# A window-attention and FFT-filter block on one core: attention weights divided ahead of the transpose, heads laid out by GpSimd's transfers

## The chip, the cores and the metric

The kernel runs on one core of a Trainium2 chip. The metric is the device time of one execution in microseconds (us); of several executions the median is given. A core has five engines that work side by side: TensorE (PE, matrix multiplications; PEld is its load of the stationary operand), VectorE (DVE), ScalarE (ACT), GpSimd (POOL) and SyncE (SP, which here only issues transfers). Everything is float32.

## What is computed

The input x has 8 images of 384 channels and 64x64 pixels. Two blocks follow each other, each added to its input:

```python
# block 1: windowed attention
xt = layernorm(groupnorm(x) as tokens of 384 channels) * norm_g + norm_b
qkv = xt @ qkv_w + qkv_b                       # q, k, v of 384 channels each
# channels 0..191: branch 0; channels 192..383: branch 1, the image rolled by (-4, -4)
# each branch: 8x8 windows of 64 tokens, 4 heads of 48 channels
attn = q @ k.T * 48**-0.5 + bias[head]         # branch 1: and a mask
out_b = softmax(attn) @ v                      # branch 1 is rolled back
x = x + concat(out_0, out_1) @ proj_w + proj_b
# block 2: filter
t = w_in @ groupnorm(x)                        # per pixel, 384 to 384
t = irfft2(rfft2(8x8 patches of t) * fft_filter)
t = depthwise_conv3x3(t, w_dw)
x = x + w_out @ (gelu(t[:192]) * t[192:])
```

The group norms need statistics over a whole image (32 groups of 12 channels).

## The kernel before

**Strips and units.** An image is cut into 8 strips of 8 rows, 512 tokens. A strip has two units, one for each branch (`br`), so an image has 16 units. The attention strip `s` of image `b` starts at unit u = 16b + 2s, its branch `br` at w = u + br. Block 2 of image b ("conv stage") runs beside the attention of image b+1: its strip s starts at u = 16(b+1) + 2 + 2s. For the last image nothing is left beside it, and this is the tail of the program.

**The plan.** A list of pieces is written by `at(place, piece, ...)` (L832 and after for attention), sorted by place, and run in that order. TensorE executes its instructions just as written (`keep_in_program_order` in the helpers `matmul`, L62, and `transpose`, L72). The instructions of the other engines are ordered by a scheduler when the program is built, within dependencies and the pins that the program sets (`behind`, `keep_in_program_order`). Empty instructions on TensorE (`nop`, counted in `FETCHES`, `WAITS` and `RUN_AT`) align the places at which instructions are fetched.

**PSUM.** Two pools: "gemm", four buffers of 128x512, and "att", two buffers of 128x2x512 (`psum2`). "att" is taken in turn by the scores pS, the transposed weights pT, the weighted values pA, the turned output po, and by pw2, the third output of `finish`. The matrix multiplication that first writes a buffer waits until the readers of its previous holder are done.

**One unit of attention, with the lines.**

- `group_normal` (L338, DVE) writes y; `ln_square` (L347) squares it on ACT into sq, and POOL adds the three parts of sq (L350); `ln_sums` sums over channels on PE, ACT and DVE turn the sums into factors (L362 to L367, among them ACT's Sqrt), these go through a line in DRAM and come back spread over all partitions as rs (L374, L376, SP's queue); `ln_scale` (L389, DVE) multiplies. POOL makes the half-shifted copy of y for branch 1 (L402 to L404).
- `qk_tile`: products pq, moved by ACT to qab, kab, qcd, kcd (L420). Heads lie at 64 rows each.
- `v_tile`: pvv, copied by ACT to v (L454). v has 49 columns per head, the last is set to one by POOL (L445).
- `scores`: pS, 32 products of 64x64. `weights` (DVE): bias added (L482), maximum (L486), subtraction (L489). `exponent` (ACT, L495). `turn`: eight transposes into pT, one ACT copy eT (L505).
- `apply`: eT stationary (64x64), v moving (49 columns): pA has tokens on its partitions, and the 49th column of each head is the sum of the weights. `normalise` (DVE): reciprocal of the sums (L529) and product o (L530).
- `put`: eight transposes of o into po (with the identity or one that swaps halves), and copies by ACT and DVE into oT, which has channels on partitions (L553, L554, L561 to L563; branch 1, the shifted one, goes in two halves to two strips).
- `project`: pr from oT and proj_w, added by DVE to x_add (L572). `keep` takes statistics (L247), `store` writes the result of block 1 to DRAM (SP).

**One strip of the conv stage.** `normal_x1` (ACT, L600), `mix` (pt, copied by ACT at L610), `transform` (pf, multiplied by the filter on DVE, L627), `back` (pz, 96 products). Then `border` once for each of three channel tiles: ACT copies pz into z, which has a border of one pixel (L655), and the border rows between neighbouring strips (L658 reads pz, L659 reads z). `conv`: nine taps; the first by ACT (L695), eight by DVE (L701, with zz as the running sum). `gate`: Gelu on ACT and products on DVE (L714 to L718). `finish`: products pw into two "gemm" buffers and pw2, in this order on PE, sixteen of 64 rows and then four of 128; DVE adds them to x_finish (L740 to L742), SP stores.

**The order around a finish.** On PE a strip's `back` (unit u + 1.99), the `apply` of branch 1 (w + 1.00), the next `scores` (w + 0.05) and a `finish` of an earlier conv strip (u + 6.10) follow each other: pz, pA, pS, pw. Of the "att" buffers, pS takes the one that pT held, pw2 the one that pA held.

Of the kernel before, what the change touches and what calls it, by code (L numbers as in the profile page):

```python
# [7 lines left out]
F32 = mybir.dt.float32  # L8
AF = mybir.ActivationFunctionType
ALU = mybir.AluOpType  # L10
# [17 lines left out]
C_SWAP = C_PICK + 2  # L28
N_CONST = C_SWAP + 128
WAITS = 5.325, -22  # L30
FETCHES = {"qk_tile": 12, "v_tile": 24, "project": 12, "scores": 128, "apply": 128, "turn": 16, "put": 16,
# [7 lines left out]
def block_kernel(ctx: ExitStack, tc: tile.TileContext, out, x, consts, fsel, wqk, wv, bqk, bv,  # L39
# [52 lines left out]
    swap = cst[:, C_SWAP:C_SWAP + P]  # L92
# [6 lines left out]
    nc.vector.memset(eps_t, LN_EPS)  # L99
    std_t = cp.tile([P, 1], F32, name="std_t")  # L100
# [193 lines left out]
    for z in z_bufs:  # L294
        nc.gpsimd.memset(z[:, :, 0:1], 0.0)
        nc.gpsimd.memset(z[:, :, SW + 1:SW + 2], 0.0)
    gs0, gs1, st0s, st1s, x1d = ({} for _ in range(5))

    def behind(i, other, kind, reason):
        tc.add_manual_dep(i.ins, other.ins.name, mybir.DependencyInfo(kind, mybir.DependencyReason.DATA),  # L300
                          reason=reason)

# [49 lines left out]
    def ln_sums(b, s):  # L352
# [10 lines left out]
        rc = sb.tile([P, P], F32, tag="lr", bufs=2, name=f"lr_{b}_{s}")  # L363
        nc.vector.tensor_tensor(rc, m[:, 0:P], m[:, 0:P], ALU.mult)  # L364
        nc.vector.tensor_tensor(rc, m[:, P:2 * P], rc, ALU.subtract)
        nc.scalar.activation(rc, rc, AF.Sqrt, bias=eps_t)
# [19 lines left out]
    def ln_scale(b, s):  # L386

        y, rs = ys[b, s], ys.pop((b, s, "rs"))
        nc.vector.tensor_tensor(y, y, rs.unsqueeze(1).to_broadcast([P, KC, ST]), ALU.mult)  # L389
# [50 lines left out]
    def v_tile(b, s, br, g):  # L440

        y = y2s[b, s] if br else ys[b, s]
        if g == 0:
            v = sb.tile([P, 4, 4, HD + 1], F32, tag="v", bufs=2, name=f"v_{b}_{s}_{br}")
            nc.gpsimd.memset(v[:, :, :, HD:HD + 1], 1.0)  # L445
            vs[b, s, br] = v
        v = vs[b, s, br]
        pvv = psum(f"pvv_{b}_{s}_{br}_{g}")
        for i in range(2):
            pair = 2 * g + i  # L450
            for k in range(KC):
                matmul(pvv[:, i * 192:(i + 1) * 192], y[:, k, pair * P:(pair + 1) * P],
                                 wv_sb[:, k, br * 192:(br + 1) * 192], start=(k == 0), stop=(k == KC - 1))
        nc.scalar.copy(v[:, 2 * g:2 * g + 2, :, 0:HD],  # L454
                       pvv[:, 0:384].rearrange("p (g h d) -> p g h d", g=2, h=4))
# [17 lines left out]
    def weights(b, s, br):  # L473
# [13 lines left out]
        if br == 0 and "added" in zs:  # L487
            behind(i, zs.pop("added"), mybir.DependencyClass.NoSync, "residual first")
        zs["soft"] = nc.vector.tensor_tensor(e, e, mx.unsqueeze(2).to_broadcast([P, 2 * NS, 64]),  # L489
                                             ALU.subtract)  # L490
        qks[b, s, br, "e"] = e

    def exponent(b, s, br):
        e = qks[b, s, br, "e"]
        nc.scalar.activation(e, e, AF.Exp)  # L495

# [11 lines left out]
    def apply(b, s, br):  # L508

        eT, v = qks.pop((b, s, br, "eT")), vs.pop((b, s, br))  # L510
        pA = psum2(f"pA_{b}_{s}_{br}")
        for i in range(2):
            for h in range(4):
                to = (i * 4 + h) * (HD + 1)
                for odd in range(2):
                    pair = 2 * i + odd
                    for q in range(2):
                        rows, half = slice(q * 64, (q + 1) * 64), (q + odd) % 2
                        col = pair * P + (h + q) % 2 * 64
                        matmul(pA[half * 64:(half + 1) * 64, odd, to:to + HD + 1],  # L520
                               eT[rows, h // 2, col:col + 64], v[rows, pair, h, :], start=True, stop=True)
        qks[b, s, br, "A"] = pA

    def normalise(b, s, br):
        nm = f"{b}_{s}_{br}"
        o = os_[b, s, br] = sb.tile([P, 2, 2, 192], F32, tag="o", bufs=1, name=f"o_{nm}")
        pA = qks.pop((b, s, br, "A"))[:, :, 0:8 * (HD + 1)].rearrange("p g (h d) -> p g h d", h=8)
        rc = small.tile([P, 2, 8], F32, tag="rc", bufs=2, name=f"rc_{nm}")
        nc.vector.reciprocal(rc.unsqueeze(3), pA[:, :, :, HD:HD + 1])  # L529
        nc.vector.tensor_tensor(  # L530
            o.rearrange("p g i (h d) -> p g (i h) d", d=HD),
            pA[:, :, :, 0:HD], rc.unsqueeze(3).to_broadcast([P, 2, 8, HD]), ALU.mult)
# [6 lines left out]

    def put(b, s, br):  # L540


        o = os_.pop((b, s, br))
        p = psum2(f"po_{b}_{s}_{br}")
        po = []
        for a in range(2):
            for pair in range(4):
                transpose(p[:, a, pair * P:(pair + 1) * P], o[:, pair % 2, pair // 2, a * 64:a * 64 + P],
                          swap if pair % 2 else ident)
            po.append(p[:, a].rearrange("p (w r c) -> p r w c", w=NS, r=WS))  # L550
        if br == 0:
            oT = out_tile(b, s)
            nc.scalar.copy(oT[:, 0].rearrange("p r (w c) -> p r w c", c=WS), po[0])  # L553
            nc.vector.tensor_copy(oT[64:P, 1].rearrange("p r (w c) -> p r w c", c=WS), po[1][64:P])  # L554
            return
        for half, oT in ((0, out_tile(b, s)), (1, out_tile(b, (s + 1) % NS))):
            to, of = slice(4 - 4 * half, 8 - 4 * half), slice(4 * half, 4 * half + 4)
            for rows, kt, src, copy in ((slice(0, 64), 1, po[0], nc.vector.tensor_copy),
                                        (slice(0, P), 2, po[1], nc.scalar.copy)):
                d = oT[rows, kt, to]  # L560
                copy(d[:, :, 4:60].rearrange("p r (w c) -> p r w c", c=WS), src[rows, of, 0:7])  # L561
                copy(d[:, :, 60:64], src[rows, of, 7, 0:4])
# [408 lines left out]
```

## Time and profile before

The time before is 3689.26 us, the median of 3 runs (3688.66 to 3691.13). The profiled execution took 3687.27 us; its span, from the first to the last instruction in the trace, is 3685.3 us, and TensorE's granted clock was 0.996 of full speed. The figures below are of this one execution.

| from the views of the profile | value |
| --- | --- |
| profiled execution, span | 3687.27 us, 3685.3 us |
| window 1500 to 2000 us: PE busy | 496.86 us |
| the same: DVE, ACT, POOL busy | 399.99, 336.88, 59.62 us |
| DVE zz L701 | 1483 instructions, 1076.1 us, mean 751 ns |
| DVE x_add L572 | 192, 143.4 us, mean 747 ns |
| ACT oT L553, 128x512 | 64, 37.5 us, mean 585 ns |
| ACT z L655 | 192, 125.9 us, mean 672 ns |
| ACT loads of a function table | 72 counted at L495, 92.4 us, mean 1283 ns |
| POOL DMA issue L175, 2 KB | 64, 35.8 us, mean 582 ns; 5.5 us from issue to landing |

How to read the lines of the profile: a group has the source line, the engine, the operation, what it writes and from what, partitions x elements and type, and the number of records (a float32 product that isn't a transpose leaves two on PE); after the bar the busy time in us and the mean of one in ns; after the second bar the engine's idle time just before the group and what ended most of it. In the timeline the columns are the start in us, the length in us, the group and, in brackets, the idle time before it and what ended it. Matrix products are pipelined, so their lengths overlap: what a group costs is read from its start to the start of the next. In the view of waits a line has engine, operand and line of the waiting instruction, what it waited for, and the sum, the number and the longest of the waits.

### The profile page before, as it was taken

What the parts mean: (1) busy time and instruction counts of PE and PEld (TensorE: products, weight loads), DVE (VectorE), ACT (ScalarE), POOL (GpSimd) and SP (SyncE); (2) the same over time, 40 slices, a digit from 0 to 9 for tenths busy, and PEclk for the clock granted to TensorE, in tenths of its full rate; (3) what the DMA queues carried; (4) which work ended last, traced back from release to release, by engine and by line L of the source; (5) the groups of instructions that cost most, each with busy time, mean ns of one, the idle gap of its engine ahead of it and who ended that gap; (6) DMA issues with size and microseconds to landing.
All of it is one profiled execution on the core that took longest, in us unless ns stands there. A gap on an engine that the chain in (4) does not pass through costs nothing.

```text
span 3685.3 us, 92936 instructions
## 1 busy us (share of the span) xinstructions
PE 3610.8 (98%) x38598; PEld 2340.3 (64%) x38598; DVE 2836.7 (77%) x4601; ACT 2382.5 (65%) x3947; POOL 426.1 (12%) x764
## 2 busy tenths in 40 slices
PE   6999999999999999999999999999999999999998
PEld 4666666666666666666666666666666666666554
DVE  5655578778878788877888778878788777777898
ACT  3776576667666576666766766666676666676442
POOL 4111011101111011111111111111011111100000
PEclk8999999999999999999999999999999999999999
DMA  4232223223323133323332322323232322221432
GB/s 121 87 101 81 76 96 126 85 90 121 124 90 106 70 133 123 105 81 118 118 107 93 112 97 104 133 81 110 87 130 102 109 90 85 100 82 69 159 112 78
DMA packets 144355, 377.07 MB, mean 102 GB/s; under 512 B 12288, under 2 KB 12876, under 8 KB 143948
## 3 DMA queue, kind: packets, MB, share of 16 engines
q1 hardware_dynamic: 139952, 370.60, 28.5%
q8 instruction: 319, 5.23, 0.6%
q0 software_dynamic: 2048, 0.15, 0.1%
q10 hardware_dynamic: 1948, 0.37, 0.1%
q14 instruction: 88, 0.72, 0.1%
HBM read 270.28 MB, written 100.79 MB: 101 GB/s over the span
## 4 chain that ended last, share of the span: by engine, by line
PE 86%; DVE 6%; DMA 3%; ACT 2%; issue 1%; ACTq 0%; SPq 0%; DVEq 0%
PE pq L62 25%; PE pr L62 13%; PE pvv L62 12%; PE pt L62 12%; PE pw L62 6%; DVE zz L701 3%; PE pS L62 3%; PE pA L62 3%; PE po L72 3%; PE pT L72 3%; PE pz L62 3%; PE pf L62 2%; PE ln L62 2%; DMA x_norm<-in_x_dram 1%; DMA rs<-line 1%
## 5 line engine op out<-in xcount | busy, mean ns | idle before, releaser
L701 DVE SCALAR_TENSOR_TENSOR zz<-z,dw_sb,zz 128x512 f32<-128x512 f32 x1483 | 1076.1, 751 | 23.1 <-ACT z L658 11.0
L62 PE MATMUL pq<-y,wqk_sb 128*128 128x512 f32 x2160 | 990.1, 596 | 0.0
L62 PEld LDWEIGHTS pq<-y,wqk_sb 128*128 128x128 f32 x2160 | 402.3, 190 | 436.6 <-issue 403.4
L62 PE MATMUL pt<-wi_sb,xn 128*128 128x384 f32 x1536 | 535.0, 486 | 1.0 <-ACT xn L600 1.0
L62 PE MATMUL pr<-oT,wp_sb 128*128 128x512 f32 x1152 | 523.1, 592 | 0.9 <-DVE oT L563 0.9
L62 PE MATMUL pvv<-wv_sb,y 128*128 128x192 f32 x2880 | 495.8, 326 | 0.0
L62 PEld LDWEIGHTS pvv<-wv_sb,y 128*128 128x128 f32 x2880 | 471.7, 190 | 36.2 <-issue 22.2
L420 ACT ACTIVATE qab<-pq,bq_sb,cst 96x512 f32<-96x512 f32 (+1 forms) x256 | 197.8, 773 | 383.0 <-PE pq L62 381.1
L62 PEld LDWEIGHTS pt<-wi_sb,xn 128*128 128x128 f32 x1536 | 285.9, 190 | 202.7 <-issue 43.3
L420 ACT ACTIVATE kcd<-pq,vec 32x512 f32<-32x512 f32 x512 | 348.4, 680 | 9.0
L62 PEld LDWEIGHTS pr<-oT,wp_sb 128*128 128x128 f32 x1152 | 211.1, 190 | 224.3 <-issue 213.5
L402 POOL COPY y<-y 128x384 f32<-128x384 f32 x112 | 100.0, 893 | 1525.0 <-PE pvv L62 1020.5
L610 ACT COPY t<-pt 128x384 f32<-128x384 f32 x256 | 124.2, 485 | 186.0 <-PE pt L62 182.8
L364 DVE TENSOR_TENSOR lr<-m 128x128 f32<-128x128 f32 x64 | 18.9, 295 | 281.6 <-ACT m L362 281.6
L695 ACT ACTIVATE zz<-z,dw_sb 128x512 f32<-128x512 f32 x182 | 133.1, 733 | 151.0 <-PE pw L62 139.2
L350 POOL TENSOR_TENSOR sq<-sq 128x512 f32<-128x512 f32 x122 | 156.4, 1282 | 627.4 <-ACT sq L347 622.6
L420 ACT ACTIVATE qcd<-pq,bq_sb,cst 96x512 f32<-96x512 f32 (+1 forms) x256 | 197.1, 770 | 45.6 <-PE pq L62 42.1
L454 ACT COPY v<-pvv 128x384 f32<-128x384 f32 x256 | 120.8, 477 | 157.6 <-PE pvv L62 156.9
L572 DVE SCALAR_TENSOR_TENSOR x_add<-pr,vec,x_add 128x512 f32<-128x512 f32 x192 | 143.4, 747 | 93.3 <-PE pr L62 91.5
L62 PE MATMUL pw<-zz,wo_sb 128*128 128x512 f32 (+1 forms) x512 | 182.2, 499 | 0.0
L420 ACT ACTIVATE kab<-pq,vec 96x512 f32<-96x512 f32 (+1 forms) x256 | 174.1, 680 | 8.5 <-PE pq L62 6.8
L72 PEld LDWEIGHTS pT<-cst,e 128*128 128x128 f32 x1024 | 119.1, 141 | 67.8 <-issue 39.3
(142 smaller groups left out, 5292.4 us busy)
## 6 DMA issues: line engine op xcount, KB each, us to landing
x_add<-in_x_dram SPq DMA_DIRECT2D x64, 768.0 KB, 9.7
x1d<-x_add SPq DMA_DIRECT2D x64, 768.0 KB, 3.7
x_mix<-x1d SPq DMA_DIRECT2D x64, 768.0 KB, 4.6
x_finish<-x1d SPq DMA_DIRECT2D x64, 768.0 KB, 5.8
out_dram<-x_finish SPq DMA_DIRECT2D x64, 768.0 KB, 3.8
x_norm<-in_x_dram SPq DMA_DIRECT2D x61, 768.0 KB, 7.6
x_stats<-in_x_dram SPq DMA_DIRECT2D x56, 768.0 KB, 7.8
rs<-line SPq DMA_DIRECT2D x62, 256.0 KB, 3.0
```

The source lines that it names most:

```text
L62: tc.keep_in_program_order(nc.tensor.matmul(*args, **kw))
L72: tc.keep_in_program_order(nc.tensor.transpose(*args, **kw))
L350: nc.gpsimd.tensor_tensor(sq[:, 0, :], sq[:, 0, :], sq[:, k, :], ALU.add)
L364: nc.vector.tensor_tensor(rc, m[:, 0:P], m[:, 0:P], ALU.mult)
L402: nc.gpsimd.tensor_copy(dst[:, :, :, :, 0:4], src[:, :, :, :, 4:8])
L420: return nc.scalar.activation(dst[to:to + n], pq[of:of + n], AF.Identity, bias=bias[of:of + n], scale=scale)
L454: nc.scalar.copy(v[:, 2 * g:2 * g + 2, :, 0:HD], pvv[:, 0:384].rearrange("p (g h d) -> p g h d", g=2, h=4))
L572: nc.vector.scalar_tensor_tensor(t[:, m, :], pr, bp_sb[:, m:m + 1], t[:, m, :], ALU.add, ALU.add)
L610: nc.scalar.copy(t1, pt[:, 0:C])
L695: nc.scalar.activation(zz.rearrange("p (r c) -> p r c", c=SW), z[:, 1:9, 1:SW + 1], AF.Copy, scale=dw_sb[:, m, 4:5])
L701: i = nc.vector.scalar_tensor_tensor(acc.rearrange("p (r c) -> p r c", c=SW), z[:, dy:dy + 8, dx:dx + SW], dw_sb[:, m, TAPS[tap]:TAPS[tap] ...
```

## The change

- `divide` is new, on DVE after `exponent`: the sum over each row of e, its reciprocal, and the product. `normalise` is gone, and with it v's column of ones: v is contiguous, 768 columns and 16 of padding, in one fixed buffer per branch.
- `apply` makes v stationary (64 columns: the 48 of a head and 16 of what comes after it) and eT moving (64 columns). pA then has channels on its partitions, two heads per tile at rows 0 and 64. The 16 columns over give rows that nobody reads.
- `put` has no transposes. ACT copies pA into o (branch 0: two copies of 512 columns; branch 1: 512, 384, 64 and 64), and GpSimd issues transfers that move each head's 48 rows from o to their place in oT: five for branch 0, ten for branch 1, where a head may be cut at the edge of a tile.
- `border` is split: `inner` copies pz into z, for tiles 0 and 2 in `back`, for tile 1 in `borders` at u + 2.08, where all border rows are copied too, now both from z.
- Orders are fixed. `after_softmax` puts `ln_scale`, the sums of `project` and all taps of `conv` (except for the last image) behind the newest softmax on DVE; `after_out` puts the border copies and the first tap on ACT behind the last o copy of a branch 1. A one-column Exp right after the Sqrt of `ln_sums` brings the table of Exp early.
- Places in the plan: exponent from 0.30 to 0.13, divide at 0.23 or 0.26, turn from 0.64 to 0.80, put from 1.23 to 1.07. The buffer lr is single. The swapping matrix is gone; `WAITS` has new numbers.

```diff
@@ -28,4 +28,3 @@
-C_SWAP = C_PICK + 2
-N_CONST = C_SWAP + 128
-WAITS = 5.325, -22
-FETCHES = {"qk_tile": 12, "v_tile": 24, "project": 12, "scores": 128, "apply": 128, "turn": 16, "put": 16,
+N_CONST = C_PICK + 2
+WAITS = 5.97, -31
+FETCHES = {"qk_tile": 12, "v_tile": 24, "project": 12, "scores": 128, "apply": 128, "turn": 16,
@@ -99,0 +98 @@
+    exp_t = cp.tile([P, 1], F32, name="exp_t")
@@ -296,0 +296,4 @@
+    v_bufs = [cp.tile([P, 16 * HD + 16], F32, name=f"v{i}") for i in range(2)]
+    for v in v_bufs:
+        nc.gpsimd.memset(v[:, 16 * HD:], 0.0)
@@ -302,0 +306,4 @@
+    def after_softmax(i):
+        if "soft" in zs:
+            behind(i, zs["soft"], mybir.DependencyClass.NoSync, "softmax first")
@@ -363 +370 @@
-        rc = sb.tile([P, P], F32, tag="lr", bufs=2, name=f"lr_{b}_{s}")
+        rc = sb.tile([P, P], F32, tag="lr", bufs=1, name=f"lr_{b}_{s}")
@@ -366 +373,3 @@
-        nc.scalar.activation(rc, rc, AF.Sqrt, bias=eps_t)
+        i = nc.scalar.activation(rc, rc, AF.Sqrt, bias=eps_t)
+        behind(nc.scalar.activation(exp_t, eps_t, AF.Exp), i, mybir.DependencyClass.NoSync, "table in time")
@@ -389 +398 @@
-        nc.vector.tensor_tensor(y, y, rs.unsqueeze(1).to_broadcast([P, KC, ST]), ALU.mult)
+        after_softmax(nc.vector.tensor_tensor(y, y, rs.unsqueeze(1).to_broadcast([P, KC, ST]), ALU.mult))
@@ -444,3 +454 @@
-            v = sb.tile([P, 4, 4, HD + 1], F32, tag="v", bufs=2, name=f"v_{b}_{s}_{br}")
-            nc.gpsimd.memset(v[:, :, :, HD:HD + 1], 1.0)
-            vs[b, s, br] = v
+            vs[b, s, br] = v_bufs[br]
@@ -454,2 +462 @@
-        nc.scalar.copy(v[:, 2 * g:2 * g + 2, :, 0:HD],
-                       pvv[:, 0:384].rearrange("p (g h d) -> p g h d", g=2, h=4))
+        nc.scalar.copy(v[:, 384 * g:384 * (g + 1)], pvv[:, 0:384])
@@ -489,2 +496,2 @@
-        zs["soft"] = nc.vector.tensor_tensor(e, e, mx.unsqueeze(2).to_broadcast([P, 2 * NS, 64]),
-                                             ALU.subtract)
+        zs.pop("soft", None)
+        nc.vector.tensor_tensor(e, e, mx.unsqueeze(2).to_broadcast([P, 2 * NS, 64]), ALU.subtract)
@@ -496,0 +504,7 @@
+    def divide(b, s, br):
+        e = qks[b, s, br, "e"]
+        rc = small.tile([P, 2 * NS], F32, tag="rc", bufs=2, name=f"rc_{b}_{s}_{br}")
+        nc.vector.tensor_reduce(rc, e, AX.X, ALU.add)
+        nc.vector.reciprocal(rc, rc)
+        zs["soft"] = nc.vector.tensor_tensor(e, e, rc.unsqueeze(2).to_broadcast([P, 2 * NS, 64]), ALU.mult)
@@ -512,10 +527,8 @@
-        for i in range(2):
-            for h in range(4):
-                to = (i * 4 + h) * (HD + 1)
-                for odd in range(2):
...
+        for hp in range(2):
+            for pair in range(4):
+                to = (hp * 4 + pair) * 64
+                for par, q in ((0, 0), (1, 1), (0, 1), (1, 0)):
+                    rows, of = slice(q * 64, (q + 1) * 64), (pair * 4 + hp * 2 + par) * HD
+                    col = pair * P + (par + q) % 2 * 64
+                    matmul(pA[par * 64:(par + 1) * 64, q, to:to + 64], v[rows, of:of + 64],
+                           eT[rows, hp, col:col + 64], start=True, stop=True)
@@ -524,10 +536,0 @@
-    def normalise(b, s, br):
-        nm = f"{b}_{s}_{br}"
-        o = os_[b, s, br] = sb.tile([P, 2, 2, 192], F32, tag="o", bufs=1, name=f"o_{nm}")
-        pA = qks.pop((b, s, br, "A"))[:, :, 0:8 * (HD + 1)].rearrange("p g (h d) -> p g h d", h=8)
...
@@ -539,0 +543,4 @@
+    def after_out(i):
+        if "out" in zs:
+            behind(i, zs["out"], mybir.DependencyClass.NoSync, "weighted values first")
@@ -543,8 +550,7 @@
-        o = os_.pop((b, s, br))
-        p = psum2(f"po_{b}_{s}_{br}")
-        po = []
-        for a in range(2):
...
+        pA = qks.pop((b, s, br, "A")).rearrange("p o (h w r c) -> p o h w r c", h=2, w=4, r=WS)
+        o = sb.tile([P, 2, ST], F32, tag="o", bufs=1, name=f"o_{b}_{s}_{br}")
+        def columns(first, n, step=16, c=WS):
+            return bass.AP(o.tensor, o.offset + first, [list(o.ap[0]), [ST, 2], [step, n], [SW, WS], [1, c]])
@@ -552,12 +558,19 @@
-            oT = out_tile(b, s)
-            nc.scalar.copy(oT[:, 0].rearrange("p r (w c) -> p r w c", c=WS), po[0])
-            nc.vector.tensor_copy(oT[64:P, 1].rearrange("p r (w c) -> p r w c", c=WS), po[1][64:P])
-            return
...
+            for q in range(2):
+                nc.scalar.copy(columns(q * WS, 4), pA[:, q])
+            parts = ((slice(0, WS), 0, out_tile(b, s)),)
+        else:
+            nc.scalar.copy(columns(4, 4), pA[:, 0])
+            nc.scalar.copy(columns(12, 3), pA[:, 1, :, 0:3])
+            nc.scalar.copy(columns(60, 1, c=4), pA[:, 1, :, 3:4, :, 0:4])
+            zs["out"] = nc.scalar.copy(columns(0, 1, c=4), pA[:, 1, :, 3:4, :, 4:8])
+            parts = ((slice(4, 8), 0, out_tile(b, s)), (slice(0, 4), 256, out_tile(b, (s + 1) % NS)))
+        edge = (P, 64)[br]
+        for rows, of, oT in parts:
+            n = (rows.stop - rows.start) * SW
+            for h in range(4):
+                row = h % 2 * 64 - h * HD
+                for a, z in ((h * HD, min((h + 1) * HD, edge)), (max(h * HD, edge), (h + 1) * HD)):
+                    if a < z:
+                        to = a + br * P + (64 if a >= edge else 0)
+                        nc.gpsimd.dma_start(out=oT[to % P:to % P + z - a, to // P, rows],
+                                            in_=o[row + a:row + z, h // 2, of:of + n])
@@ -572 +585,2 @@
-        nc.vector.scalar_tensor_tensor(t[:, m, :], pr, bp_sb[:, m:m + 1], t[:, m, :], ALU.add, ALU.add)
+        after_softmax(nc.vector.scalar_tensor_tensor(t[:, m, :], pr, bp_sb[:, m:m + 1], t[:, m, :],
+                                                     ALU.add, ALU.add))
@@ -644,2 +658,3 @@
-        for m in (0, 2, 1):
-            border(b, s, m, pz[m])
+        zs[b, s, "pz"] = pz
+        for m in (0, 2):
+            inner(b, s, m)
@@ -647 +662 @@
-    def border(b, s, m, pz):
+    def inner(b, s, m):
@@ -654,6 +669,2 @@
-        rows = by_window(pz)
-        nc.scalar.activation(z[:, 1:9, 1:SW + 1].rearrange("p r (w c) -> p w r c", c=WS), rows, AF.Copy)
-        if s:
-            above = zs[b, s - 1, m]
...
+        nc.scalar.activation(z[:, 1:9, 1:SW + 1].rearrange("p r (w c) -> p w r c", c=WS),
+                             by_window(zs[b, s, "pz"][m]), AF.Copy)
@@ -661,0 +673,8 @@
+    def borders(b, s):
+        inner(b, s, 1)
+        for m in (0, 2, 1) if s else ():
+            above, z = zs[b, s - 1, m], zs[b, s, m]
+            after_out(nc.scalar.copy(above[:, WS + 1, 1:SW + 1], z[:, 1, 1:SW + 1]))
+            after_out(nc.scalar.copy(z[:, 0, 1:SW + 1], above[:, WS, 1:SW + 1]))
@@ -695,2 +714,2 @@
-                nc.scalar.activation(zz.rearrange("p (r c) -> p r c", c=SW), z[:, 1:9, 1:SW + 1], AF.Copy,
-                                     scale=dw_sb[:, m, 4:5])
+                after_out(nc.scalar.activation(zz.rearrange("p (r c) -> p r c", c=SW), z[:, 1:9, 1:SW + 1],
+                                               AF.Copy, scale=dw_sb[:, m, 4:5]))
@@ -707,2 +726,2 @@
-        if b < B - 1 and (tap == 6 or m == 0 and tap == 1):
-            behind(i, zs["soft"], mybir.DependencyClass.NoSync, "softmax first")
+        if b < B - 1:
+            after_softmax(i)
@@ -797,2 +816,4 @@
-                at(w + 0.30, exponent, b, s, br)
-                at(w + 0.64, turn, b, s, br)
+                at(w + 0.13, exponent, b, s, br)
+                at(w + (0.23, 0.26)[br], divide, b, s, br)
+                at(w + 0.80, turn, b, s, br)
@@ -800,2 +821 @@
-                at(w + 1.07, normalise, b, s, br)
-                at(w + 1.23, put, b, s, br)
+                at(w + 1.07, put, b, s, br)
@@ -827,0 +848 @@
+            at(u + 2.08 if b < B - 1 or s < NS - 1 else u + 1.991, borders, b, s)
@@ -831 +852 @@
-                    at(u + (2.62, 3.15, 3.5)[n] + 0.06 * tap, conv, b, s, m, tap)
+                    at(u + (2.62, 3.10, 3.5)[n] + 0.05 * tap + (0.4 if n == 2 and tap > 3 else 0), conv, b, s, m, tap)
```

## The prediction, made before the changed kernel was run

> **What bounds the kernel now.** I read the page's busy line and chain first, then the lines by shape (who does the removed and added work), then the waits between 500 and 3430 us (the repeating part), last the timeline at one finish.
>
> ```profile
> PE 3610.8 (98%) x38598; PEld 2340.3 (64%) x38598; DVE 2836.7 (77%) x4601; ACT 2382.5 (65%) x3947; POOL 426.1 (12%) x764
> PE 86%; DVE 6%; DMA 3%; ACT 2%; issue 1%; ACTq 0%; SPq 0%; DVEq 0%
> ```
> TensorE is busy for 98% and carries 86% of the chain. DVE has 23% free, ACT 35%, POOL 88%. A microsecond taken off PE counts; one put on the others counts only where PE waits for it.
>
> ```profile
> L72 PE MATMUL po<-cst,o 128*128 128x128 f32 x1024 | 133.0, 273 | 0.0
> L62 PE MATMUL pA<-v,eT 64*64 64x49 f32 x8192 | 146.6, 218 | 1.3 <-issue 0.8 <-ACT eT L505 0.5
> L62 PE MATMUL pS<-kab,qab 64*64 64x64 f32 x4096 | 89.1, 219 | 0.8 <-issue 0.7
> L62 PE MATMUL pS<-kcd,qcd 64*64 64x64 f32 x4096 | 86.8, 218 | 0.3 <-issue 0.3
> L489 DVE TENSOR_TENSOR e<-e,mx 128x1024 f32<-128x1024 f32 x128 | 158.5, 1238 | 2.7
> L486 DVE TENSOR_REDUCE mx<-e 128x16 f32<-128x1024 f32 x128 | 155.5, 1215 | 2.4
> L530 DVE TENSOR_TENSOR o<-pA,rc 128x768 f32<-128x768 f32 x128 | 122.5, 957 | 4.3
> L347 ACT ACTIVATE sq<-y 128x1536 f32<-128x1536 f32 x64 | 95.1, 1486 | 55.6 <-DVE y L338 55.4
> ```
> These are groups by line and shape: busy us, mean ns of one, idle before. The first row goes; pA becomes as wide as the two pS rows; the subtraction and maximum price the new division; the last row matters below: sq waits on ACT for DVE's normalisation y.
>
> ```profile
> PE pT L72 <- ACT e L495: 7.8, 7, 1.4
> PE pz L62 <- ACT v L454: 6.6, 12, 1.0
> PE pw L62 <- DVE o L530: 4.0, 6, 1.0
> ```
> PE's waits in the repeating part: 18.4 us with 0.7 of issue. The third is the place to watch: pw2, finish's third output, takes the PSUM buffer of the "att" pair that pA held, and waits for pA's reader.
>
> ```profile
> 1804.43 1.04 PE L72 MATMUL po<-cst,o 128*128 128x128 f32 x8
> 1805.31 2.10 PE L62 MATMUL pt<-wi_sb,xn 128*128 128x384 f32 x6
> ...
> 1848.70 2.02 PE L62 MATMUL pz<-cst,t 64*64 64x64 f32 x94
> ...
> 1852.48 1.69 PE L62 MATMUL pw<-g,wo_sb 64*64 64x512 f32 x16
> ```
> From start to start po takes 0.88 us of PE. From pz's start T to pw's first is 3.78 us; eight pw matmuls more (1.08 us) and 0.08 put pw2's first at T+4.94.
>
> **What the skill says.** "PSUM — Partial Sum Buffer", Engine vs sequencer instructions: the queues of ScalarE, VectorE and GpSimdE are strict FIFO. The trace agrees: a copy of v waiting only for pvv stood behind sq until 1851.50. "Perfetto Trace Analysis", Identifying the Most-Contended Engine: matmul busy misleads because matmuls are pipelined. Agrees: po is 133.0 us busy, 128×0.88=112.6 start to start; I use the latter. "ScalarE: Activation LUTs", What ACT_TABLE_LOAD costs: about 1283 ns a load; the trace has 1283. "DMA: Bandwidth & Descriptors", Anatomy of one DMA — SWDGE: 2.0 us and bytes/436e3, so 2.2 us for the new 98 KB transfers, an estimate; the trace has no such transfer, only 2 KB ones issued by POOL, 0.58 us each and 5.5 to landing at the loaded start.
>
> **Part by part.**
>
> 1. po's transposes: 128 units × 0.88 = **−112.6 us** of PE, all on the path.
>
> 2. pA, 49 to 64 columns: start to start 0.92–0.97 before, pS of 64 columns 1.00–1.04; 0.08×128 = **+10 us**. Bounds: 0, and 29 by busy (89.1+86.8−146.6).
>
> 3. DVE: loses rc and o (29.8+122.5) and its oT copies (64×0.695 + 128×0.378 + 256×0.157 = 133): 285 us. Gains a reduction (1.22), a reciprocal (0.2) and a multiplication (1.24) of 128x1024 per unit: 337. Net +52, 79% busy: cover is left. In one unit, behind Exp: 2.6 us more between scores and what follows.
>
> 4. ACT: loses the oT copies of four lines (groups of 37.5, 43.2, 22.7 and 24.2, together 128 us); gains o, in branch 0 two copies of 512 columns at 0.585, in branch 1 four of 512, 384, 64 and 64, so about 1.2–1.3 us per unit, 160; and 64 Exp of one column that bring the table early (the built program has 200 loads of a table for 198, so it moves them and adds almost none). Net +40, beside PE except as in 7. The line buffer lr goes from two to one; its readers are done a whole strip earlier: nothing.
>
> 5. POOL: loses 128 small memsets, gains 15 DMAs a strip, 960 × 0.57 = 550 us on an engine at 12%. They go by POOL's own queue; SP issues the same loads and stores in the same order. Cover: ten of the shifted branch take 5.7 us to issue, up to 5.5 to land, perhaps 2 of queueing: 13 us. Put is at u+2.07, project at u+3.27, 29 us. The following o is written over 20 us later. Cost nothing, once 1.5–3 us at the last strip. Bounds 0 to 25: POOL's shifted copies and sq additions queue behind the issues, and ln sums waits for these.
>
> 6. More empty PE instructions (3794 to 5403) stand in the dense qk and project stretches: nothing, bound 5. The softmax-first pins order DVE as it must run anyway.
>
> 7. **The new wait.** pA used to be released by DVE's o, 1.2 us after pA, due at once. Now it is released by ACT's four o copies, ending 1.27 after they start, and these stand, in the order in which the changed program lists ACT's instructions, behind the strip's three z copies (0.54 each) and in most strips behind sq, which waits for DVE's y. With T the start of pz:
>  - Strips 2, 3: DVE from the end of pS P: start at P+0.8; bias 1.37, maximum 1.24, subtraction 1.14, three zz 2.3, division 2.6, three x_add, seven zz and three statistics of x_add at 0.67–0.75, three of x_stats 1.8, ln_scale 1.7, y 1.45: 22.2–22.4, so P+23.0–23.2. P to T was 21.3 (1827.40 to 1848.70), now 20.4 without po: y ends at T+2.6–2.8 (T+1.32 before). With T+2.6: 0.1, sq 1.39, z 1.62, o 1.27, 0.1 of release: T+7.09. PE waits 2.15 in each.
>  - Strip 1: sq stands after z; no projection in the unit, so T is only P+12.5; y by the same sum P+19.3 = T+6.8; sq and o: T+9.66. Wait 4.7.
>  - Strip 0: the order is z, z, two of xn, z, o; xn waits for the shift of the new image: o ends at about T+8.5. Wait 3.6.
>  - Strips 4–7: y ends at T+0.8 (their x_stats are done); 0.1+1.39+v 0.36+1.62+1.27+0.1: T+5.65. Wait 0.75.
>  Per image 3.6+4.7+2×2.15+4×0.75 = 15.6. Conv runs beside attention fully in images 2–6 (78), image 7 has 13.4, image 1 strips 3–7 only, 5.2: **+96.6 us** over 52 finishes, 1.86 each. As the trace of before has no such wait, the bounds are 0 and 1.86+1.
>
> 8. Waits that go: pT has 0.3–0.5 of a unit more after Exp, pz loses the v wait: **−18.4**; in strip 0 pT may wait for the longer chain, +2.8.
>
> 9. Tail, last image, DVE-bound: border rows stand behind two inner copies, 0.6 × 7 = **+4**.
>
> Sum: −112.6+10+96.6−18.4+2.8+4 = **−17.6**. Against the profiled 3687.3: 3669.7. The median of the runs before is 2.0 above their profiled execution: 3671.
>
> **Rivals.**
>
> A. The o copies are in time (y earlier than I sum, or ACT faster): all but 7 stands. 3687.3−112.6+10−18.4+2.8+4+2 = **3575**; with a wait only in strips 0 and 1 (about 45 us) 3620. For: DVE has 21% free and ACT 33. Against: four instructions in one FIFO behind a DVE result that already came 2.72 us after ACT was ready (the sq at 1850.11).
>
> C. Slower. Same place, the finish's pw2: DVE's y is late by 1 us more in each strip (a zz waiting for a border copy, the division waiting for Exp, which stands behind moves of q and k on ACT). Each us is 52 on the path: 3671+52 = **3723**. It decides from 17.6/52 = 0.34 us more, an average wait of 2.2 instead of 1.86. For: added up from the same rows, DVE's work and waits in a strip with x_stats take 54.0 of the 55.6 us that PE would then need, so lateness is regained slowly. Against: PE's own waiting gives DVE time.
>
> D. The change doesn't hide its transfers: GpSimd's ten DMAs take 29 us or o's next write waits. pr waits for them, 0.4 us in 48 strips: 3671+20 = **3691**. For: nothing but the 5.5 us landing at 2 KB; against: 16 us of margin.
>
> **How the numbers follow.** Forecast 0.46 (3645 to 3695 as its own range), A 0.22, C 0.24, D 0.08. The predicted time is 3671. Unknowns: pA 0 to +29 around 10, the wait ±52, POOL 0 to 25. The range reaches into A to 3590, leaving out the fullest saving (0.11), and into C to 3715, leaving out about 0.08. What a measurement can tell from no change is 0.2%, 7.4 us: below 3681.9 or above 3696.6. Faster: A 0.22, 0.37 of the forecast, 0.01 of C, 0.02 of D: 0.62. Within: 0.08+0.02+0.02 = 0.12. Slower: 0.01+0.21+0.04 = 0.26.
>
> **What would show it.** No po row; pA start to start near 1.02; TensorE busy some 100 less while the span falls by less. PE waits of pw for ACT's o copies: near 97 us in the forecast, none in A, above 115 in C; and within them strip 1 longest. ACT's sq after DVE y should idle more than 55 us. No PE wait of pr for a DMA, unless D. Step 3 is wrong if DVE is the one that PE waits for at pT or at pf; step 6 if matmul groups grow by issue gaps. The forecast fails above all if o stands on ACT where its order isn't the one that decides, that is, if y is ready earlier than these sums.

## The result, and the profile after

The changed kernel takes 3664.91 us, the median of 4 runs (3664.11 to 3665.57), beside 3688.96 us (3688.61 to 3691.13, 4 runs) for the kernel before in the same series: a ratio of 0.9933, 95% interval 0.9916 to 0.9951. The prediction had 3671, in a range of 3590 to 3715. The span of the profiled execution is 3662.7 us against 3685.3, so 22.6 us less where the sum of the prediction was 17.6 less.

From the page of the changed kernel, its busy line, the chain that ended last and GpSimd's costliest line:

```profile
PE 3525.8 (96%) x37574; PEld 2236.5 (61%) x37574; DVE 2903.4 (79%) x4281; ACT 2462.4 (67%) x3949; POOL 885.7 (24%) x1598
...
PE 76%; DVE 11%; ACT 5%; issue 2%; DMA 0%; ACTq 0%; SPq 0%; DVEq 0%
...
L575 POOL DMA_DIRECT2D oT<-o x960 | 482.0, 509 | 600.8 <-ACT o L559 456.5
```

TensorE is busy 85 us less (the prediction said some 100), but the span is only 22.6 us shorter: its idle time rose from 74.5 to 136.9 us. The chain has gone from 86% TensorE to 76%, with DVE and ACT in its place. The lines of the changed program by shape, and TensorE's waits over the whole run, say where:

```profile
L61 PE MATMUL pA<-eT,v 64*64 64x64 f32 x8192 | 152.7, 220 | 16.2 <-issue 11.8 <-ACT eT L519 4.3
L61 PE MATMUL pw<-g,wo_sb 64*64 64x256 f32 x512 | 43.8, 404 | 52.4 <-ACT o L565 52.0
L354 ACT ACTIVATE sq<-y 128x1536 f32<-128x1536 f32 x64 | 95.1, 1486 | 90.7 <-DVE y L345 90.5
```
```profile
PE pw L61 <- ACT o L565: 52.0, 45, 3.6
PE pz L61 <- DVE t L641: 12.0, 15, 2.5
...
PE pA L61 <- issue: 11.8, 12, 1.3
PE pT L71 <- DVE e L509: 6.6, 7, 1.1
```

The row of po is gone. The new wait is where the prediction put it, pw2 behind ACT's o copies (L562 to L565), 45 times, and ACT's sq idles 90.5 us for DVE's y where it idled 55.4 before. The recorded 52.0 us are not all of it: records of the products ahead of the wait are longer too. A measure that doesn't depend on where records end is the time from a finish's first pw to the next group of products. Where nothing waits it is 4.13 us, so I call what is above 4.13 the excess of a finish. Summed over the 52 finishes that have attention beside them it is 9.8 us before and 80.7 after:

| strip of attention beside the finish | before, us per finish | after, us per finish | wait forecast, us |
| --- | --- | --- | --- |
| 0 | 0.45 to 1.26 | 1.68 to 2.09 | 3.6 |
| 1 | 0.32 to 0.66 | 2.78 to 5.31 | 4.7 |
| 2, 3 (images 2 to 6) | up to 0.22 | 1.66 to 1.90 | 2.15 |
| 4 to 7 (images 2 to 6) | 0 | 0.17 to 1.09 | 0.75 |

Two finishes outside the table stand out, and the prediction had neither so high: the first one of the program with 4.93 us (beside strip 3 of image 1) and one with 4.67 (beside strip 4 of image 7), where six instructions that write `taps`, 1.84 us on ACT, stand between z and o.

How it comes about is read from one finish of strip 2, in the timeline of the changed kernel, DVE's last y, then ACT, then TensorE:

```profile
1837.25 1.45 DVE L345 TENSOR_SCALAR y<-x_norm,gs_a 128x512 f32<-128x512 f32 x3
```
```profile
1838.80 1.49 ACT L354 ACTIVATE sq<-y 128x1536 f32<-128x1536 f32 x1 [1.65 <-DVE y L345]
1840.19 1.69 ACT L669 ACTIVATE z<-pz 128x512 f32<-128x512 f32 x3
1841.74 0.60 ACT L562 COPY o<-pA 128x512 f32<-128x512 f32 x1
...
1842.67 0.28 ACT L565 COPY o<-pA 128x64 f32<-128x64 f32 x1
```
```profile
1836.55 2.02 PE L61 MATMUL pz<-cst,t 64*64 64x64 f32 x94
...
1840.34 1.63 PE L61 MATMUL pw<-g,wo_sb 64*64 64x512 f32 x8
1843.01 0.66 PE L61 MATMUL pw<-g,wo_sb 64*64 64x256 f32 x8 [1.04 <-ACT o L565]
```

ACT is idle for 1.65 us because sq heads its queue and y isn't there; the z copies behind it start only after it, though pz is under way since 1836.55. The excess of this finish is 1.8 us. With T = 1836.55, y is done at about T+2.2, o at T+6.4, pw2 starts at T+6.46. The prediction had T+2.6, T+7.0 and T+7.09.

### The profile page after: what moved, and what is told of

Its sections match the earlier page's. It is cut to its first block, busy times and chain, and to the rows that moved or that the text cites. A ratio compares the mean times of both kernels' runs of the same rounds, so it can differ in the third digit from the quotient of the medians.

```text
span 3662.7 us, 93502 instructions
## 1 busy us (share of the span) xinstructions
PE 3525.8 (96%) x37574; PEld 2236.5 (61%) x37574; DVE 2903.4 (79%) x4281; ACT 2462.4 (67%) x3949; POOL 885.7 (24%) x1598
## 4 chain that ended last, share of the span: by engine, by line
PE 76%; DVE 11%; ACT 5%; issue 2%; DMA 0%; ACTq 0%; SPq 0%; DVEq 0%
PE pq L61 23%; PE pr L61 13%; PE pvv L61 11%; PE pt L61 11%; DVE zz L720 5%; PE pw L61 5%; PE pA L61 3%; PE pz L61 3%; PE pT L71 3%; PE pf L61 2%; PE pS L61 2%; ACT z L669 2%; PE ln L61 1%; DVE t L641 1%; DVE st L246 1%
## 5 line engine op out<-in xcount | busy, mean ns | idle before, releaser
L575 POOL DMA_DIRECT2D oT<-o x960 | 482.0, 509 | 600.8 <-ACT o L559 456.5
L61 PE MATMUL pvv<-wv_sb,y 128*128 128x192 f32 x2880 | 508.1, 326 | 0.9 <-ACT kcd L429 0.9
L411 POOL COPY y<-y 128x384 f32<-128x384 f32 x112 | 82.3, 735 | 1243.9 <-PE pvv L61 753.5
L61 PEld LDWEIGHTS pr<-oT,wp_sb 128*128 128x128 f32 x1152 | 218.6, 190 | 268.6 <-issue 245.9
L507 DVE TENSOR_REDUCE rc<-e 128x16 f32<-128x1024 f32 x128 | 155.8, 1217 | 86.7 <-ACT e L502 86.7
L61 PE MATMUL pw<-zz,wo_sb 128*128 128x512 f32 (+1 forms) x512 | 189.9, 515 | 0.0
```

The costliest lines, as they stand in the source:

```text
L61: tc.keep_in_program_order(nc.tensor.matmul(*args, **kw))
L411: nc.gpsimd.tensor_copy(dst[:, :, :, :, 0:4], src[:, :, :, :, 4:8])
L507: nc.vector.tensor_reduce(rc, e, AX.X, ALU.add)
L575: nc.gpsimd.dma_start(out=oT[to % P:to % P + z - a, to // P, rows], in_=o[row + a:row + z, h // 2, of:of + n])
```

## The experiments

All twelve are edits of the changed kernel, each beside runs of the kernel before on the same chip. A time is a median, a ratio is to the kernel before, with its 95% interval. Excess and gaps are read from the one execution that was profiled. "Issue gaps" are TensorE's idle times that the profile puts down to issue; in pA and pS they are 13.6 us in the changed kernel.

| run | us | ratio | excess of 52 finishes, us | issue gaps in pA, pS, pq, pw, us |
| --- | --- | --- | --- | --- |
| before | 3688.96 | 1 | 9.8 | 1.8 |
| changed | 3664.91 | 0.9933 (0.9916 to 0.9951) | 80.7 | 13.6 |
| e1 sq after o | 3595.86 | 0.9743 (0.9728 to 0.9757) | 16.0 | 13.5 |
| e2 sq and xn after o | 3612.19 | 0.9791 (0.9775 to 0.9807) | 13.3 | 18.4 |
| e3 finish later | 3626.36 | 0.9829 (0.9812 to 0.9845) | 3.0 | 26.0 |
| e4 branch 1 not divided | 3610.06 | 0.9780 (0.9765 to 0.9795) | 32.9 | 6.7 |
| e5 transfers twice | 3800.46 | 1.0300 (1.0277 to 1.0323) | 161.3 | 23.5 |
| e6 old transposes back | 3742.40 | 1.0148 (1.0122 to 1.0174) | 42.1 | 22.9 |
| e7 six transfers | 3680.49 | 0.9974 (0.9964 to 0.9984) | 67.9 | 31.9 |
| e8 old WAITS | 3677.71 | 0.9969 (0.9963 to 0.9976) | 95.5 | 34.4 |
| e10 sq, first xn after o | 3591.18 | 0.9735 (0.9720 to 0.9749) | 3.9 | 13.3 |
| e11 sq after o, shifted | 3590.63 | 0.9735 (0.9719 to 0.9752) | 14.4 | 14.3 |
| e12 six transfers, aligned | 3671.73 | 0.9957 (0.9942 to 0.9972) | 98.5 | 10.6 |
| e13 e10 and e11 together | 3592.19 | 0.9734 (0.9720 to 0.9747) | 2.6 | 12.1 |

### e1: is it the order on ACT?

```diff
-        nc.scalar.activation(sq, ys[b, s], AF.Square)
+        after_out(nc.scalar.activation(sq, ys[b, s], AF.Square))
```

> The changed kernel with one pin more: ScalarE's squares sq stand behind the o copies of branch 1. Theory (finish's pw2 waits for o, and o waits behind sq, which waits for DVE's y): o then follows the z copies, ends by about T+4.3 and pw2, due at T+4.94, waits only in strip 0. Finishes, measured in the changed kernel at 4.13 us and up, fall back to 4.13 in strips 1 to 7; their excess of 80.7 us over 52 finishes falls to about 15, so 3665-66 = 3600 us. Rival 1 (the o copies are late because of the z copies and their own length): the excess stays above 50, time 3640 or more. Rival 2 (the wait moves: sq, 3 us later, makes the ln sums or the moves of q and k late): pw no longer waits but ln or pS does, time above 3630.

Measured 3595.86 us, 69 us less than the changed kernel (0.9743 against 0.9933 of the kernel before), with an excess of 16.0 us, of which 13.5 is in strip 0. The same place of strip 2 in its timeline, ACT and then TensorE:

```profile
1800.38 1.73 ACT L669 ACTIVATE z<-pz 128x512 f32<-128x512 f32 x3 [0.63 <-PE pz L61]
1802.31 0.59 ACT L562 COPY o<-pA 128x512 f32<-128x512 f32 x1 [0.20 <-PE pA L61]
...
1803.27 0.24 ACT L565 COPY o<-pA 128x64 f32<-128x64 f32 x1
...
1804.42 1.48 ACT L354 ACTIVATE sq<-y 128x1536 f32<-128x1536 f32 x1
```
```profile
1799.17 2.02 PE L61 MATMUL pz<-cst,t 64*64 64x64 f32 x94
...
1802.90 1.51 PE L61 MATMUL pw<-g,wo_sb 64*64 64x512 f32 x16
1804.34 2.85 PE L61 MATMUL pw<-zz,wo_sb 128*128 128x512 f32 x8
```

ACT now waits for TensorE's pz and pA, not for DVE; o is done at T+4.3, and all sixteen pw run through. sq is done at T+6.7 (T+3.7 in the changed kernel), and nothing on TensorE waits for it. The order on ACT is shown to be the cause of the wait in strips 1 to 7; both rivals fall.

### e2 and e10: the rest in strip 0

e2, on top of e1, puts all of xn behind o; e10 only the xn of the first conv strip:

```diff
+            after_out(i)                       # e10: if s == 0 and b < B - 1
-            at(u + 0.02, normal_x1, b, s)
+            at(u + 0.075, normal_x1, b, s)     # e10: for those strips alone
```

> As the kernel with sq behind o, and the normalised input xn of the conv stage behind o too (its place in the plan from u + 0.02 to u + 0.075). Theory: strip 0, where xn waits for the shift of a new image ahead of o, loses its excess of about 2 us as well, 6 finishes: 12 us less than the run with sq alone, about 3588. Rival: xn is then late for the first pt, which waits in each strip: PE waits of pt for xn of 1 us and more in 50 strips, slower than the run with sq alone.

> The kernel with sq behind o, and xn behind o in the first strip of the conv stage alone. Theory: the first finish of an image loses most of its excess of 13.5 us in 6 finishes, with no late pt in the other strips: 3596-9 = 3587. Rival: the first pt waits for xn in its place, 3596 or more.

e2 is 16 us slower than e1, though its excess is lower (13.3), and not in the way that the rival said: pt waits for xn once, 1.0 us. TensorE instead waits a little at many places: pw for issue 8.2 us, pq for DVE's filter product 5.7, pt and pq for ACT's kcd 8.5, pt for x_add 2.4. What links these is not settled. e10 lowers the excess to 3.9 us. Its time is 4.7 us below e1's, but the ratios (0.9735 and 0.9743) lie inside each other's intervals, so a gain over e1 isn't shown.

### e3: another way to give o time

```diff
-            at(u + 6.10, finish, b, s)
+            at(u + 6.15, finish, b, s)
```

> The changed kernel with finish put one piece later in the plan (u + 6.10 to u + 6.15), behind the first three matrix products pq of the next unit, about 2.6 us of TensorE; the order on ScalarE (sq ahead of o) stays. Theory (what costs is only that pw2 comes before ACT has done o): pw2 is due at T+7.5, o ends by T+5.7 to T+7.1 in strips 2 to 7, by T+6.9 in strip 0 and by T+9.7 in strip 1; of the excess of 80.7 us some 12 are left in strip 1; time about 3600. Rival (the lateness sits in DVE's and ACT's loop of a strip, and comes out somewhere else): PE waits instead at pz, pT, ln or pq, and the time stays above 3640.

The excess goes almost wholly, from 80.7 to 3.0 us, without a change to the order of sq and o: it is the date of pw2 against the date of o that counts. But the time falls by only 38.5 of these 77.7 us. Issue gaps rise by 12.4 us (pq 8.8, pS 8.1, pA 9.2), groups of pq take 14.6 us more from start to start, those of pS 5.7. Between both forecasts, then: the wait is understood, and moving a piece of TensorE's program brought back half of it elsewhere.

### e4: is DVE's division the reason that y is late?

```diff
...
-                at(w + (0.23, 0.26)[br], divide, b, s, br)
+                if br == 0:
+                    at(w + 0.23, divide, b, s, br)
```

> Branch 1 leaves out the division of its weights (reduction, reciprocal, product; DVE is 2.6 us shorter between its scores and y). Theory: y, sq and with them o come 2.6 us earlier, so the excess of a finish falls by 2 to 2.6 in strip 1, to 0 in strips 2 to 7, and stays in strip 0: about 50 to 55 us of the 80.7, time 3612. Rival (o is late by ACT's own copies, whatever y does): the excess stays near 80 and the time at 3660 to 3665.

3610.06 us, and the excess falls by 47.8 us to 32.9: nothing is left in strips 2 to 7 but 1.5 us at the last image, 10.1 in strip 0 and 21.4 in strip 1 (about 5.2 us each in images 2 to 4, no less than in the changed kernel, and about 2 in the other three; 2 to 2.6 less was expected everywhere). The rival falls for strips 2 to 7.

In strip 1 the wait did become shorter: in images 2 to 4 TensorE's recorded idle time in the finish is 2.04 to 2.40 us where it was 3.28 to 3.65. But it comes in two pieces, because the z copies stand behind sq too, and pw's second buffer waits for them:

```profile
PE pw L61 <- ACT o L567: 16.1, 13, 2.1
...
PE pw L61 <- ACT z L671: 3.6, 3, 1.4
```

Right after the second wait of these three finishes, and in no other finish of this run that has attention beside it, TensorE's clock stands at half for 3.41 us, which adds about 1.7 us to the work of the finish (last section). Waits of 2.0 to 2.4 us, 1.7 of clock, and longer records ahead of both waits make up the 5 us.

### e6: the first term of the sum

```diff
...
+    def old_turn(b, s, br):
+        p, o = psum(f"po_{b}_{s}_{br}"), os_.pop((b, s, br))
+        for i in range(8):
+            transpose(p[:, i % 4 * P:(i % 4 + 1) * P], o[:, i // 4, i % 4 * P:(i % 4 + 1) * P], ident)
...
```

> The changed kernel with the eight transposes of each unit put back on TensorE at their old place, of o, into a PSUM buffer that nobody reads. By the prediction's first term they cost 0.88 us each unit, 112.6 in all. Theory of the wait: those of branch 0 stand between the scores and pz, so T comes 0.88 us later while y does not, and the excess falls by 0.88 in strips 1, 2 and 3 and by 0.5 in strips 4 to 7, some 30 us; together 3665+113-30 = 3748. Rival (the wait has nothing to do with the distance of y from T): the whole 113 us, 3778.

3742.40 us (3734 to 3756). The excess falls by 38.6 us (30 expected), above all in strips 2 to 7. 112.6−38.6 and 9 us more of issue gaps make 83, against 77.5 measured. So half of the new wait is bought by the very transposes that were removed: without them T, and with it pw2, comes earlier while y does not.

### e5, e7, e12: do GpSimd's transfers cost anything?

e5 wraps the `dma_start` in `for _ in range(2)`. e7 moves whole ranges of rows, six transfers a strip; e12 is e7 with `WAITS = 4.9, -31`:

```diff
+        whole = ((slice(0, P), 0), (slice(64, P), 1)) if br == 0 else ((slice(0, 64), 1), (slice(0, P), 2))
...
+            for i, (p, kt) in enumerate(whole):
+                nc.gpsimd.dma_start(out=oT[p, kt, rows], in_=o[p, i, of:of + n])
```

> Each of GpSimd's transfers from o to oT is issued twice, 1920 instead of 960. Theory: they lie beside the other work with 16 us of margin; the ten of branch 1 then take about 10 us to issue and 4 to land, still inside 29 us; time 3665 to 3672, no PE wait of pr for a transfer. Rival (the transfers are close to the path, by oT's arrival or by o's buffer or by POOL's other work behind them): 20 us or more slower, with waits of pr for oT, of ACT's o for a transfer, or of ln for sq.

> The changed kernel with six transfers a strip in place of fifteen, which move as many rows from o to oT but not to the places that the heads belong to (the padding rows go along, the layout of heads in oT is left out). Forecast of the prediction's step 5 (960 transfers beside the other work cost nothing): 3660 to 3668. Rival, after the run with each transfer twice was 135 us slower (GpSimd's queue is close to the path through its shifted copies and sums of sq, or the transfers slow the loads of x that y waits for): faster by 10 us or more, 3655 or less, and the excess of the finishes falls.

> The kernel with six transfers a strip (heads not at their places in oT) again, with WAITS 4.9, -31 in place of 5.97, -31: in its first run 32 us of issue gaps in pA and pS moved along the program by about 1.07 counts a unit, so its TensorE has that many fewer waiting instructions a unit than the number 5.97 stands for. Theory (960 transfers cost nothing beside the other work, and the first run was slower by these gaps alone): gaps back to 10 to 15 us, time 3680-20 = 3660, between 3650 and 3668. Rival (the fewer, wider transfers are slower by themselves): 3675 or more. Rival (fifteen transfers cost something): below 3645.

e5 is 135 us slower. But it doesn't test what it was made for: the second copy writes where the first does, and GpSimd waits for it to land. Its waits in e5:

```profile
POOL oT L576 <- DMA oT<-o: 756.6, 270, 9.9
```

So GpSimd's queue grows not by 480 us of issues alone but by 757 of waiting. What is behind it comes late: pq waits 6.6 us for the shifted y, ln 3.6 for sq; loads of x_norm take 10.2 us to land instead of 7.6, the excess doubles, and the clock is lower (last section). It shows that this queue can come onto the path, not that it is on it.

e7 was 15.6 us slower with fewer transfers, and its gaps told why: from strip to strip the gap stood a little later in TensorE's program. At 841 us the row of pA that follows it in the timeline has 27 records; at 3338 us the gap has wandered into pS, with 12 records in the row of its first half. The kernel aligns places of TensorE's program by counting, and with fewer transfers fewer waiting instructions stand on TensorE than the count supposes. With the count set for it (e12) the rows of pA after the gaps have 43 to 49 records throughout, and 21 of 32 us are gone.

The time of e12, 3671.73 us (3669 to 3678), is 4 us above the expected range; it is not below the changed kernel's. Its excess, 98.5 us, is that of the longest of its executions. That one is 13.8 us longer than the changed kernel's profiled one, with 17.9 us more excess and 3.0 less of issue gaps, 14.9 together; so about 1 us is left that fewer transfers could have saved. (Of the larger excess about 9 us is the clock, which at half speed loses 17.1 us in e12's finishes and 8.5 in the changed kernel's; the rest is longer waits that were not followed up.) Nine transfers a strip fewer save next to nothing: the 960 are hidden, as the prediction had it.

### e8 and e11: what are the issue gaps?

e8 is the changed kernel with the old `WAITS = 5.325, -22`; e11 is e1 with

```diff
-WAITS = 5.97, -31
+WAITS = 5.97, -15
```

> The changed kernel with the numbers WAITS of the kernel before (5.325, -22), so only the count of empty instructions on TensorE differs. Step 6 of the prediction took these as nothing. Theory: the 12 waits 'pA <- issue' of the changed kernel (11.8 us) are places where TensorE's instructions come late, and with the old numbers there are more of them, 50 or more, in pA, pS, pz and pw: 3690 to 3720. Rival (these issue gaps have another cause): within 5 us of 3665.

> The kernel with sq behind o, with WAITS 5.97, -15 in place of 5.97, -31: 16 fewer counts at each aligned place of TensorE's program. Theory (the gaps in pA stand at a fixed count of TensorE's instructions, where these are fetched): they move by 16 counts, 8 records, from 43 records of pA left to 35; their size stays about 1 us each, and the time within 8 us of 3596. Rival (they come from a wait for data): they stay at 43 left.

With the old numbers the gaps grow to 34.4 us and wander through pA, pw and pS, in most strips from 1957 us on; the median is 12.8 us above the changed kernel's, less than expected (3690 to 3720; the profiled execution was 3692, the longest of 20). In e11 the gaps move by just the 16 counts: the row of pA after each of the eleven gaps has 42 to 44 records in e1 and 34 to 36 in e11, their sum is 11.3 and 11.4 us (two counts make one record). They stand at a fixed count of TensorE's instructions and wait for no data. That an instruction is fetched late there is what the names in the kernel suppose; no record shows the fetch. Why they appear in the pA ahead of strips 0 and 1 and not of the others stays open.

### e13: the two together

The edits of e10 and e11, in one kernel.

> The two edits that helped beside sq behind o together: xn of the first strip behind o, and WAITS 5.97, -15. They act at different places (the first finish of an image; the pieces between scores and qk), so if both gains are real (5.2 and 4.7 us against the run with sq alone) they add: 3586, with a finish excess of 3 to 5 us and pA gaps at 35 records left. Rival (the runs differ by chance or the shift's gain was the same time counted twice): 3589 to 3592.

3592.19 us, ratio 0.9734: no better than either. The rival holds: that the differences of 5 us to e1, which ran in another series, are gains isn't shown. e1 is the edit that counts, 2.6% below the kernel before and 1.9% below the changed one (0.9743/0.9933).

## Why the prediction was right, and where its terms were off

| step of the prediction | forecast, us | profile before to after, us |
| --- | --- | --- |
| 1. po | −112.6 | −112.0 |
| 2. pA | +10 | +5.0 |
| 7, and 8's wait of pw | +96.6−4.0 | +69.2 (idle +48.0, longer pw groups +21.2) |
| 8. waits of pT and pz | −14.4+2.8 | −10.6; new waits for DVE's t and ACT's eT +7.6 |
| 6. issue gaps | 0, bound 5 | +11.8 |
| 5. transfers | 0, +1.5 to 3 at the end | no PE wait of pr for them |
| 9. tail | +4 | +3.9 (21.4 us a strip where it was 20.85, seven times) |
| sum | −17.6 | −25.1 of these; span −22.6 |

- **Steps 1, 5 and 9** came out as worked: po, the hidden transfers and the tail. That the start-to-start cost, not the busy time, is what is won with po is shown twice, by the profile and by e6.
- **Step 2** was half of its estimate: pA takes 0.97 us a unit from start to start (123.7/128), not 1.0, against 0.93 before.
- **Steps 3 and 4** were too small: DVE is busy 67 us more where +52 was worked out (2.66×128 is 340, not 337), ACT 80 more where +40 was. The o copies alone are 171 us and not 160, and the one-column Exp, priced at nearly nothing, is 13. Whether the new waits in step 8 come of it wasn't tried.
- **Step 7**, the main one, had its mechanism right (e1, e3, e4, e6) and its size 23 us too large, in each strip a little, most in strip 0. In strip 2 y came 0.4 us earlier than summed, and the four o copies took 1.21 us instead of 1.27. Strip 0 was furthest off, 2.0 for 3.6: o was done at T+7.7 where T+8.5 was taken, and an issue gap of 0.84 us in pA put pw itself later, so that it waited less. In strip 1 dates were right to 0.15 us (pw2 at T+9.53 for T+9.66), but an issue gap of 1.11 us put pw later here too, and the stall had a second price that the sum had not: the half clock, some 8.5 us over five finishes (last section). Without it the wait would be some 32 us below its forecast.
- **Step 8** had the waits that go about right, but new ones came that it had not: pq for DVE's t, and pA for ACT's eT, 7.6 us together.
- **Step 6** was wrong. Empty instructions were priced at nothing with a bound of 5; the gaps cost 11.8 us, and e3, e7 and e8 show 12 to 21 us more, with gaps that wander along the program. How much of the 11.8 any other count would save wasn't tried.
- **Rival C** did not come: DVE's loop had cover, and y was earlier. **D** did not come: no wait of pr for a transfer, and e12 saves next to nothing. **A** is what e1 makes of the kernel: 3596 where 3575 was worked out for no wait at all; against the 21 us between stand 16.0 of excess that is left and 13.5 of issue gaps, less the 5 by which pA was cheaper than forecast.

Four misses in the terms, −23 for the wait and −5 for pA, +12 for the gaps and +9 in step 8, leave −7.5 of the sum. That the total came within 5 us of the span's change is luck in the sizes; the path and the wait that decide it were argued and came true.

## What to carry to other kernels

When a reader of a shared buffer is moved from one engine to another, look up what stands ahead of the new reader in that engine's queue: here one square, waiting for a result that nobody needed yet, took some 65 of the 112 us that removing the transposes had won, and one pin of the order gave them back. An engine's slack doesn't help an instruction that stands behind one that waits. And where a program is aligned by counting instructions, an edit that changes the number of waits needs the count set again before its time is read: a count that didn't fit was worth 9 us between e7 and e12, and 13 between the changed kernel and e8.

## What the hardware showed that was not expected

After some of its stalls TensorE's clock drops. In strip 1 of the changed kernel, lines of the timeline:

```profile
1786.39 0.66 PE L61 MATMUL pw<-g,wo_sb 64*64 64x256 f32 x8 [3.28 <-ACT o L565]
1786.98 4.54 PE L61 MATMUL pw<-zz,wo_sb 128*128 128x512 f32 x8
1791.36 2.74 PE L61 MATMUL pq<-y,wqk_sb 128*128 128x512 f32 x6
```

The table by windows, of that stretch and of one in the tail (from:to and its length in us; busy time of PE, PEld, DVE, ACT and POOL; TensorE's granted clock; share of DMA; GB/s):

```profile
1785.00:1787.00 2.00, 0.61 (x9) 0.23 (x9) 0.00 (x0) 1.96 (x6) 1.59 (x2) 1.00 0.00 0
1787.00:1790.00 3.00, 3.00 (x9) 1.37 (x6) 0.69 (x1) 0.00 (x0) 3.00 (x6) 0.63 0.11 27
3477.41:3480.82 3.41, 3.41 (x49) 2.40 (x44) 3.38 (x7) 3.34 (x6) 0.00 (x0) 0.50 0.08 28
```

The eight products took 4.38 us instead of 2.68. In the record of the clock it is at exactly half for stretches of 3.41 us, here from 1787.81 us. Past the load at the start, the starts of these stretches in the changed kernel lie whole multiples of 3.41 us apart. Each costs dense work about 1.7 us, and five finishes have one, so by this estimate some 8.5 of the 80.7 us of excess are the clock's: three of the six strips 1, where the weight load had been idle for 4.16 to 4.22 us, once after 3.70, and at the first finish, where 1.87 and 1.93 us of idle weight load followed each other.

The length of the stall doesn't decide it. The other strips 1 kept the full clock after 3.44, 3.93 and 4.53 us of idle weight load, while the clock also dropped after shorter waits: 2.51 us of pz (the third line of the table) and 1.95 us of pA at 217 us, 2.50 us of pz in the tail of the kernel before, and 2.30 us of pw in a strip 0 of e1, at 1269 us, with the weight load idle for 2.24 to 3.18 us. The Trainium skill says in "TensorE: Matmul & The Clock Gate", Part 1: The HAM clock gate, that the clock is halved after an idle window of about 3.4 us, and that these windows run freely. The trace agrees with the half, with the 3.41 us and with windows that run freely; it does not agree that a whole window must be idle, since these waits were enough. What counts as idle stays open here. In e5, with stalls of 4 us and more in most strips 0 and 1, the mean granted clock was 0.978, for 0.994 in the changed kernel; over their spans that is an estimate of 62 us of full clock lost, part of its 135.

GpSimd's transfers of 96 KB took 3.8 us from issue to landing, more than the 2.2 estimated from the formula in "DMA: Bandwidth & Descriptors", Anatomy of one DMA — SWDGE, of the Trainium skill, and less than the 5.5 of the small ones that the trace of before shows; issuing one took 509 ns. In e7, transfers of 128 KB over 128 partitions took 2.1 us, shorter than those of 96 KB over 48.
